# Layer 2's relus moved behind the copies of the group two ahead, and the second map's weight sums moved from GpSimd to VectorE

## The chip, the cores and the metric

The kernel runs on one core of one Trainium2 chip. The metric is the time of one execution of the program on the device, in microseconds (us). The engines are named as in the profile: PE is TensorE (matrix products, with PEld for its weight loads), DVE is VectorE, ACT is ScalarE, POOL is GpSimd, SP issues most of the DMAs.

## The reference, cut to what matters

The program runs four layers over `x` of 128 x 64 x 256 values: a gated recurrent graph layer, masked attention, a graph layer with two batch norms (layer 2, counted from 0), and a three-product graph layer. Each is a residual step on the layer norm of `x`. The change touches layer 2 alone:

```python
agg = jnp.einsum('nm,bmd->bnd', A_hat, features)
x = agg.reshape(-1, d)
h = jax.nn.relu(_batchnorm(x @ W1.T + b1, g1, be1))   # 8192 tokens x 512
out = h @ W2.T + b2                                   # 8192 tokens x 256
out = _batchnorm(out, g2, be2)                        # statistics over all 8192 tokens
return out.reshape(b, n, -1)
```

Both batch norms need the statistics of all tokens before the first token can be normalized. The first norm therefore splits layer 2: the first map (`W1`) has to be finished for every token before the first relu can run, and the second map (`W2`) reads the relus.

## The kernel before, in words

The 8192 tokens are worked in 16 groups (`NG`) of 512. Activations lie with their features on the 128 partitions. A group's hidden activations after the first map are one tile `h1s[g]` of 128 x 4 x 512: four blocks `m` of 128 features each.

**First map and first norm.** `hidden` (the products of line 781, the statistics of line 792, the copy out of PSUM of line 793) ends with group 15. `bn_finish` (lines 1028 to 1052) then works block by block, on DVE except for one power on POOL: aggregate the statistics (L1036), add epsilon (L1037), raise to the power -1/2 on POOL (L1038), multiply by gamma (L1046), compute the shift (L1047). The four blocks come one after another, since the last statistics come one block after another. `n1sc` and `n1sh` are the scale and the shift of the first norm.

**The weight sums.** Groups 4 to 12 (`SEVEN_FC2`) compute the second map as a 2 x 2 block product in seven instead of eight products. This needs four sums or differences of blocks of `w2`, written into the room of `w1`, which is free once the first map is done. `sums` (line 217) makes them, before on POOL, in line 1110, issued after the last power of the first norm.

**Relus.** `activate(g)` (lines 1144 to 1150) applies scale, shift and relu in place on ACT: four instructions of 128 x 512 for a group.

**Second map, ordinary groups** (0 to 3 and 13 to 15). Eight products per group on PE (L1182) into two PSUM banks; DVE takes the statistics of each bank (L1191), ACT copies it to SBUF (`evicted`, L1188).

**Second map, groups 4 to 12** (`second_linear`, which calls `seven`). The seven products (L1131) use four PSUM banks. Products 1, 5, 6 and 7 come first. ACT copies the first two banks, L173 for product 1 and L174 for product 5. Product 2 is then accumulated into the first bank, so it waits for L173; product 3 waits for L174. DVE adds (L176, L177, L185, L189), POOL adds one block (L180), ACT evicts one (L225), and DVE takes statistics (L1174). DVE also makes four differences of the relu results for the next group (`fc2_differences`, L1123), into one set of four blocks `ts` that each group overwrites.

**Order.** Every engine runs its own instructions in a fixed order. A scheduler sets it when the program is built, from readiness and source order. `tc.issue_after(i)` puts what is recorded inside it behind instruction `i` on the same engine. At group 12 `layer3_weights` asks for the next layer's weights by DMA (L1081 to L1087), into tiles of finished groups.

Of the kernel before, what the change touches and what calls it, by code (L numbers as in the profile page):

```python
# [10 lines left out]
ALU = mybir.AluOpType  # L11
# [9 lines left out]
NG = NTOK // GN  # L21
# [17 lines left out]
def adj_preln_kernel(ctx: ExitStack, tc: tile.TileContext, x_in, adj, vec, bg0, bg1,  # L39
                     wg0, wg1, wih, whh, wqkv, w1t, w2t, l3w1, l3w2, l3w3, out):  # L40
    nc = tc.nc
# [27 lines left out]
    mhalf = const.tile([P, GT], F32, tag="mhalf", name="mhalf")  # L69
# [6 lines left out]
    vecs = const.tile([P, V_N], F32, tag="vecs", name="vecs")  # L76
# [87 lines left out]
    def seven(products, banks, p1, p5, out, end, parts=lambda b: [b]):  # L164

        ps = banks  # L170
        for i, p in zip((1, 5, 6, 7), ps):
            products[i](p, True)
        nc.scalar.copy(p1, ps[0])  # L173
        nc.scalar.copy(p5, ps[1])  # L174

        nc.vector.tensor_tensor(p1, p1, ps[2], ALU.add)  # L176
        added = nc.vector.tensor_tensor(p5, p5, ps[3], ALU.add)  # L177

        def finish():
            nc.gpsimd.tensor_tensor(out=out[1][1], in0=p1, in1=p5, op=ALU.add)  # L180
            end(1, 1, None)
            products[2](ps[0], False)
            end(0, 0, ps[0])
            products[3](ps[1], False)
            nc.vector.tensor_tensor(out[0][1], p1, ps[1], ALU.add)  # L185
            end(0, 1, None)
            products[4](ps[3], False)
            for to, p, q in zip(*(parts(b) for b in (out[1][0], p1, ps[3]))):
                last = nc.vector.tensor_tensor(to, p, q, ALU.add)  # L189
                end(1, 0, None, to)  # L190
            return last.ins

        finish.behind = added.ins
        return finish

    def each_behind(behind, i):
        return tc.issue_after(behind[i].ins) if behind else nullcontext()
# [10 lines left out]
    def sums(eng, a11, a12, a21, a22, s1, s2, s3, s4, behind=None, which=range(4)):  # L208

        ops = (  # L210
            (s1, a21, a22, ALU.add), (s2, s1, a11, ALU.subtract),
            (s3, a11, a21, ALU.subtract), (s4, a12, s2, ALU.subtract),
        )
        for i in which:
            s, p, q, op = ops[i]
            with each_behind(behind, i):
                last = eng.tensor_tensor(out=s, in0=p, in1=q, op=op)
        return last.ins
# [64 lines left out]
    with tc.tile_pool(name="lw", bufs=5) as lw:  # L283
# [6 lines left out]
        with tc.tile_pool(name="gw", bufs=1) as gw, tc.tile_pool(name="gcn", bufs=2) as gp, \  # L290
# [5 lines left out]
            for k in range(2):  # L296
                nc.sync.dma_start(
                    out=xs[0][:, 2 * k : 2 * k + 2, :], in_=x_view[:, 2 * k : 2 * k + 2, :]
# [205 lines left out]
        with tc.tile_pool(name="back", bufs=1, reuse_waits="tile") as back_pool, \  # L504
# [196 lines left out]
            for p, nk in ((1, 8), (2, 8), (3, 7), (4, 8)):  # L701
# [7 lines left out]
                for j in range(0, len(units), 2):  # L709
# [6 lines left out]
                    if j + 2 == len(units):  # L716
# [5 lines left out]
                        else:  # L722
                            w_att = weight_tile()
                            nc.sync.dma_start(
                                out=w_att[:, :, 0:768], in_=wqkv.rearrange("(c p) f -> p c f", p=P)
# [27 lines left out]
    def arena(pool):  # L753
        return pool.tile([P, 4, GN], F32, tag="arena", name="arena")
# [44 lines left out]
    with tc.tile_pool(name="att", bufs=2, reuse_waits="tile") as ap_:  # L799
# [5 lines left out]
        def queries_keys(b):  # L805


            q, k = qk = [ap_.tile([P, 2, GN], F32, tag=t, name=t, bufs=1) for t in ("q", "k")]
            p15 = ap_.tile([P, 2, 2, HN], F32, tag="p15", name="p15", bufs=1)

            def product(w, x):
                def issue(ps, first):
                    for r in range(2):
                        nc.tensor.matmul(  # L814
                            ps[:, r, :], lhsT=w[:, r * P : (r + 1) * P], rhs=x,
                            start=first and r == 0, stop=True, skip_group_check=True,
                        )

                return issue

            out = [[d[:, :, n * HN : (n + 1) * HN] for n in range(2)] for d in qk]
            finish = seven(
                sevens(wqk_blocks, b, product), [bank((P, 2, HN)) for _ in range(4)],
                p15[:, 0], p15[:, 1], out, ends_in(out, AF.Copy),
            )
            return q, k, finish
# [109 lines left out]
        last = None  # L936
        for g in range(NG):
# [12 lines left out]
            q, k, finish = queries_keys(blocks)  # L950
# [31 lines left out]
            if last is not None:  # L982
                pss = attend(eT, v_last)
# [13 lines left out]
            last = (e_next[0], ri_next, v)  # L997
# [20 lines left out]
        pss = attend(eT, v_last)  # L1018
# [4 lines left out]
    ar_left = ctx.enter_context(tc.tile_pool(name="arena_l", bufs=NG // 2 - 1, reuse_waits="tile"))  # L1023
    outs = []

    powers = []

    def bn_finish(st, n, v_0, v_g, v_b, tag, biased=True):


        scs, shs = [], []
        for m in range(n):
            mv = bp.tile([P, 2], F32, tag=f"{tag}mv{m}", name=f"{tag}mv{m}")
            sc = bp.tile([P, 1], F32, tag=f"{tag}sc{m}", name=f"{tag}sc{m}")
            sh = bp.tile([P, 1], F32, tag=f"{tag}sh{m}", name=f"{tag}sh{m}")
            nc.vector.bn_aggr(mv, st[:, m].rearrange("p g s -> p (g s)"))  # L1036
            nc.vector.tensor_scalar(sc, mv[:, 1:2], BN_EPS, None, ALU.add)  # L1037
            powers.append(nc.gpsimd.tensor_tensor(out=sc, in0=sc, in1=mhalf[:, 0:1], op=ALU.pow))  # L1038
            mean = mv[:, 0:1]

            nc.vector.tensor_scalar(
                mean, mean, vecs[:, v_0 + m : v_0 + m + 1], -1.0, ALU.add, ALU.mult
            )
            if not biased:
                nc.vector.tensor_tensor(mean, mean, vecs[:, v_0 + m : v_0 + m + 1], ALU.add)
            nc.vector.tensor_tensor(sc, sc, vecs[:, v_g + m : v_g + m + 1], ALU.mult)  # L1046
            nc.vector.scalar_tensor_tensor(  # L1047
                sh, mean, sc, vecs[:, v_b + m : v_b + m + 1], ALU.mult, ALU.add
            )
            scs.append(sc)  # L1050
            shs.append(sh)
        return scs, shs
# [4 lines left out]
    for g in range(1, NG):  # L1057
# [10 lines left out]
        if g == 3:  # L1068
            for a in range(2):
                nc.sync.dma_start(  # L1070
                    out=w2[a], in_=w2t.rearrange("(a b p) f -> a p b f", a=2, p=P)[a]
# [33 lines left out]
    SEVEN_FC2 = range(4, NG - 3)  # L1105
    fc2_a = [[w2[c][:, :, m * P : (m + 1) * P] for c in range(2)] for m in range(2)]

    fc2_s = [w1[:, :, i * P : (i + 1) * P] for i in range(4)]
    with tc.issue_after(powers[-1].ins):
        sums(nc.gpsimd, *fc2_a[0], *fc2_a[1], *fc2_s)  # L1110

    def fc2_blocks(a):
        return [
# [3 lines left out]
    def fc2_differences(a, which=range(4)):  # L1117
        (b11, b12), (b21, b22) = fc2_blocks(a)
        t1, t2, t3, t4 = ts
        ops = ((t1, b12, b11), (t3, b22, b12), (t2, b22, t1), (t4, b21, t2))  # L1120
        for i in which:
            t, p, q = ops[i]
            nc.vector.tensor_tensor(t, p, q, ALU.subtract)  # L1123
# [20 lines left out]
    def activate(g):  # L1144
        a = h1s[g]
        for m in range(4):
            nc.scalar.activation(  # L1147
                a[:, m, :], a[:, m, :], AF.Relu,
                bias=sh1[m], scale=sc1[m],
            )  # L1150

    for g in range(NG):
        a = h1s[g]
        if g not in SEVEN_FC2:
            activate(g)

        if g % 2 == 0:
            outs.append(arena(ar_right))
        o = outs[-1][:, 2 * (g % 2) : 2 * (g % 2) + 2, :]
        if g + 1 == SEVEN_FC2[0]:  # L1160
            tt = arena(ar_right).rearrange("p i (c n) -> p i c n", c=2)
            ts = [tt[:, i] for i in range(4)]
        ahead = g + 1 in SEVEN_FC2
        if g in SEVEN_FC2:
            finish = second_linear(a, o)
            if g + 2 in SEVEN_FC2:
                activate(g + 2)
            if ahead:
                fc2_differences(h1s[g + 1], range(3))
            finish()  # L1170
            if ahead:
                fc2_differences(h1s[g + 1], [3])
            for m in range(2):
                nc.vector.bn_stats(st2[:, m, g, :], o[:, m, :])  # L1174
        else:
            pss = [bank() for _ in range(2)]
            order = [(c, m) for c in range(4) for m in range(2)]
            if g == NG - 1:

                order.sort(key=lambda cm: cm[1])  # L1180
            for c, m in order:
                nc.tensor.matmul(  # L1182
                    pss[m], lhsT=w2[c // 2][:, c % 2, m * P : (m + 1) * P], rhs=a[:, c, :],
                    start=(c == 0), stop=(c == 3),
                )

            def evicted(m):
                nc.scalar.copy(o[:, m, :], pss[m])  # L1188

            for m in range(2):  # L1190
                nc.vector.bn_stats(st2[:, m, g, :], pss[m])  # L1191
                if (g, m) != (NG - 1, 1):
                    evicted(m)
            if g + 2 in SEVEN_FC2:
                activate(g + 2)
            if ahead:
                fc2_differences(h1s[g + 1])
        if g == NG - 4:
            w_three = layer3_weights()
# [255 lines left out]
    for g in range(NG + 1):  # L1455
# [10 lines left out]
        if s3 is not None:  # L1466
            pss = [bank((P, 2, D)) for _ in range(2)]
            if g == NG:
                pss = [pss, [bank((P, 2, D)) for _ in range(2)]]
# [78 lines left out]
```

## Time and profile before

| | us |
|---|---|
| median of 3 runs | 2468.98 (2467.39 to 2470.3) |
| the profiled execution's own time | 2469.3 |
| its span, first to last instruction | 2467.5 |
| PE busy | 2446.4 (99% of the span) |
| DVE busy | 1549.2 (63%) |
| ACT busy | 1141.8 (46%) |
| POOL busy | 451.7 (18%) |

Layer 2's second map lies between about 1569 and 1681 us of the span. The span begins at the first instruction and ends with the last; the remaining 1.8 us of the execution lie around it. A matrix product of fp32 data appears in the trace as two records, so a 128x512 product takes two records of about 0.43 us each.

In a timeline a row gives the start, the duration, the engine, the line, the operation, what it writes and reads, how often it occurs in a row, and in brackets how long the engine had been idle before it and which engine's instruction ended that. The durations of neighbouring instructions on one engine overlap at their ends, so the distance between two starts is shorter than the duration of one.

### The profile page before, as it was taken

How to read it: one execution, taken by the hardware profiler on the slowest of the kernel's cores; microseconds unless marked ns; L12 is line 12 of the kernel's file. 1: busy time of each engine (PE TensorE's matmuls, PEld its weight loads, DVE VectorE, ACT ScalarE, POOL GpSimd, SP SyncE). 2: the span in 40 equal slices, each digit the busy share in tenths (PEclk: the TensorE clock that was granted, in tenths of full speed). 3: DMA queues.
4: the chain of work that ended last, by engine and by line, in shares of the span. 5: the costliest groups of instructions: out<-in, count | busy, mean ns of one | idle time of the engine just before them, and what ended most of it. 6: DMA issues, size and time to landing. Idle time of an engine off the chain costs nothing.

```text
span 2467.5 us, 46706 instructions
## 1 busy us (share of the span) xinstructions
PE 2446.4 (99%) x19756; PEld 2093.4 (85%) x19756; DVE 1549.2 (63%) x2780; ACT 1141.8 (46%) x2042; POOL 451.7 (18%) x381
## 2 busy tenths in 40 slices
PE   9999999999999999999999999999999999999999
PEld 6678888889999998888888864487998898898888
DVE  6668866666566565566599986475655445454444
ACT  4557755444354443344565566754333323333332
POOL 4432211111111111121143331023111111111110
PEclk9999999999999999999999999999999999999999
DMA  3200000001000000000122110010000000000000
GB/s 128 92 2 1 1 18 1 1 1 35 1 1 1 1 1 1 1 13 1 39 71 72 45 36 1 1 60 1 10 10 19 10 10 19 10 10 10 19 10 18
DMA packets 48561, 48.03 MB, mean 19 GB/s; under 512 B 3680, under 2 KB 44768, under 8 KB 48352
## 3 DMA queue, kind: packets, MB, share of 16 engines
q1 hardware_dynamic: 47360, 44.23, 5.8%
q8 instruction: 155, 2.54, 0.4%
q10 hardware_dynamic: 992, 0.82, 0.1%
q14 instruction: 54, 0.44, 0.1%
HBM read 28.26 MB, written 8.39 MB: 15 GB/s over the span
## 4 chain that ended last, share of the span: by engine, by line
PE 87%; DVE 6%; ACT 3%; issue 1%; POOL 1%; DMA 1%; SPq 0%; DVEq 0%; POOLq 0%; ACTq 0%
PE ps L537 41%; PE ps L1348 16%; PE ps L1393 8%; PE ps L144 4%; PE ps L781 4%; PE ps L1312 3%; PE ps L480 2%; PE ps L456 2%; PE ps L1131 2%; PE ps L814 2%; ACT arena L1147 1%; PE ps L836 1%; PE ps L1182 1%; ACT arena L228 1%; POOL arena L180 1%
## 5 line engine op out<-in xcount | busy, mean ns | idle before, releaser
L537 PE MATMUL ps<-diff,s 128*128 128x256 f32 (+1 forms) x1824 | 393.5, 371 | 0.9 <-DVE diff L657 0.9
L1348 PE MATMUL ps<-arena 128*128 128x256 f32 x1792 | 392.4, 380 | 0.0
L1348 PEld LDWEIGHTS ps<-arena 128*128 128x128 f32 x1792 | 338.0, 190 | 53.9 <-issue 9.2
L537 PEld LDWEIGHTS ps<-diff,s 128*128 128x128 f32 x1824 | 345.9, 190 | 33.8 <-issue 1.6
L551 ACT ACTIVATE gates<-gates,lbias 128x512 f32<-128x512 f32 (+5 forms) x426 | 244.2, 621 | 203.0 <-DVE gates L185 147.1
L180 POOL TENSOR_TENSOR gates<-p 128x512 f32<-128x512 f32 (+1 forms) x115 | 149.7, 1301 | 878.6 <-DVE p L177 827.8
L537 PE MATMUL ps<-h,w 128*128 128x256 f32 (+1 forms) x1028 | 241.0, 371 | 0.0
L537 PE MATMUL ps<-diff,w 128*128 128x256 f32 (+1 forms) x1040 | 238.7, 370 | 0.0
L537 PEld LDWEIGHTS ps<-diff,w 128*128 128x128 f32 x1040 | 197.4, 190 | 18.2
L537 PEld LDWEIGHTS ps<-h,w 128*128 128x128 f32 x1028 | 194.7, 190 | 19.0 <-issue 0.5
L551 ACT ACTIVATE gates<-ps,lbias 128x256 f32<-128x256 f32 (+3 forms) x213 | 91.8, 477 | 247.0 <-PE ps L537 246.8
L180 POOL TENSOR_TENSOR arena<-arena 128x256 f32<-128x256 f32 (+1 forms) x73 | 82.1, 1125 | 587.6 <-DVE arena L177 587.6
L228 ACT ACTIVATE arena<-arena 128x512 f32<-128x512 f32 (+1 forms) x160 | 88.7, 582 | 193.7 <-POOL arena L180 101.6
L185 DVE TENSOR_TENSOR gates<-p,ps 128x512 f32<-128x512 f32 (+1 forms) x115 | 76.3, 664 | 119.5 <-PE ps L537 119.4
L1393 PE MATMUL ps<-arena 128*128 128x128 f32 x1280 | 149.7, 276 | 0.0
L1393 PEld LDWEIGHTS ps<-arena 128*128 128x128 f32 x1280 | 145.5, 192 | 1.1
L96 POOL TENSOR_TENSOR rstd<-rstd,mhalf 128x4 f32<-128x4 f32 (+1 forms) x66 | 65.9, 999 | 423.2 <-DVE rstd L95 416.5
L185 DVE TENSOR_TENSOR arena<-arena,ps 128x256 f32<-128x256 f32 (+1 forms) x73 | 43.5, 596 | 157.2 <-PE ps L1348 87.4
L176 DVE TENSOR_TENSOR p<-p,ps 128x512 f32<-128x512 f32 (+1 forms) x131 | 86.7, 662 | 48.9 <-PE ps L537 47.9
L537 PE MATMUL ps<-state,w 128*128 128x256 f32 (+1 forms) x512 | 116.1, 370 | 0.9 <-ACT p L173 0.8
L189 DVE TENSOR_TENSOR gates<-p,ps 128x512 f32<-128x512 f32 (+1 forms) x115 | 76.7, 667 | 63.9 <-PE ps L537 63.2
L537 PE MATMUL ps<-state,s 128*128 128x256 f32 (+1 forms) x512 | 115.8, 369 | 0.0
(192 smaller groups left out, 4115.7 us busy)
## 6 DMA issues: line engine op xcount, KB each, us to landing
x<-in_x SPq DMA_DIRECT2D x27, 512.0 KB, 4.1
v<-vt SPq DMA_DIRECT2D x128, 64.0 KB, 2.1
out<-x SPq DMA_DIRECT2D x15, 512.0 KB, 2.9
w<-in_wih SPq DMA_DIRECT2D x4, 1024.0 KB, 7.9
w<-in_whh SPq DMA_DIRECT2D x3, 1024.0 KB, 5.1
arena<-in_l3w SPq DMA_DIRECT2D x3, 1024.0 KB, 5.1
w<-in_wqkv SPq DMA_DIRECT2D x1, 768.0 KB, 4.4
x<-in_x SPq DMA_DIRECT2D x2, 256.0 KB, 3.0
```

The lines of the kernel that those rows point to most:

```text
L144: last = nc.tensor.matmul(pss[b][half * 64 : half * 64 + 64, c, t, :], lhsT=src[rows, t, col : col + 64], rhs=a2[rows, :], start=True, sto ...
L176: nc.vector.tensor_tensor(p1, p1, ps[2], ALU.add)
L180: nc.gpsimd.tensor_tensor(out=out[1][1], in0=p1, in1=p5, op=ALU.add)
L185: nc.vector.tensor_tensor(out[0][1], p1, ps[1], ALU.add)
L189: last = nc.vector.tensor_tensor(to, p, q, ALU.add)
L228: nc.scalar.activation(o, o, func)
L537: nc.tensor.matmul(ps[:, r], lhsT=wc[:, j, :], rhs=bc, start=first and r == 0 and c == 0, stop=True, skip_group_check=True,)
L551: nc.scalar.activation(o, ps, func, bias=lbias[:, col : col + 1])
L781: nc.tensor.matmul(ps, lhsT=w1[:, c, m * P : (m + 1) * P], rhs=a[:, 2 + c, :], start=(c == 0), stop=(c == 1),)
L1312: nc.tensor.matmul(ps[:, t, :], lhsT=w[:, t * P : (t + 1) * P], rhs=b, start=first and t == 0, stop=True, skip_group_check=True,)
L1348: nc.tensor.matmul(ps[:, r, :], lhsT=w[:, c, col : col + P], rhs=b[:, c, :], start=first and r == 0 and c == 0, stop=c == 1, skip_group_ch ...
L1393: nc.tensor.matmul(ps[:, t, :], lhsT=w[:, c, t * P : (t + 1) * P], rhs=b[:, c, :], start=first and t == 0 and c == 0, stop=c == 3, skip_gr ...
```

## The change

The relus of groups 0 and 1 are recorded ahead of the loop. All others are recorded two groups ahead: those of group g+2 behind the second copy out of PSUM of group g, which is L1188 in an ordinary group and L174 in a group with seven products. The second copy is kept in `finish.copied` or in `last` for that. The four weight sums go to DVE, behind the last shift of the first norm. No computation is added or left out.

```diff
-        nc.scalar.copy(p5, ps[1])
+        copied = nc.scalar.copy(p5, ps[1])
...
+        finish.copied = copied.ins
...
-            powers.append(nc.gpsimd.tensor_tensor(out=sc, in0=sc, in1=mhalf[:, 0:1], op=ALU.pow))
+            nc.gpsimd.tensor_tensor(out=sc, in0=sc, in1=mhalf[:, 0:1], op=ALU.pow)
...
-            nc.vector.scalar_tensor_tensor(
-                sh, mean, sc, vecs[:, v_b + m : v_b + m + 1], ALU.mult, ALU.add
+            shifts.append(
+                nc.vector.scalar_tensor_tensor(
+                    sh, mean, sc, vecs[:, v_b + m : v_b + m + 1], ALU.mult, ALU.add
+                )
             )
...
-    with tc.issue_after(powers[-1].ins):
-        sums(nc.gpsimd, *fc2_a[0], *fc2_a[1], *fc2_s)
+    with tc.issue_after(shifts[-1].ins):
+        sums(nc.vector, *fc2_a[0], *fc2_a[1], *fc2_s)
...
+    for g in range(2):
+        activate(g)
     for g in range(NG):
         a = h1s[g]
-        if g not in SEVEN_FC2:
-            activate(g)
...
             finish = second_linear(a, o)
-            if g + 2 in SEVEN_FC2:
+            with tc.issue_after(finish.copied):
                 activate(g + 2)
...
             def evicted(m):
-                nc.scalar.copy(o[:, m, :], pss[m])
+                return nc.scalar.copy(o[:, m, :], pss[m])
...
                 if (g, m) != (NG - 1, 1):
-                    evicted(m)
-            if g + 2 in SEVEN_FC2:
-                activate(g + 2)
+                    last = evicted(m)
+            if g + 2 < NG:
+                with tc.issue_after(last.ins):
+                    activate(g + 2)
```

More of the change, by code (lines that the diff above doesn't have):

```diff
@@ L1024, in adj_preln_kernel @@
     outs = []
-    powers = []
+    shifts = []
     def bn_finish(st, n, v_0, v_g, v_b, tag, biased=True):
```

## The prediction

> **What bounds the kernel now.** I read the shares first: PE is busy 99% of the span, so only a gap in PE counts. Then I asked which of PE's waits lie in the second map of layer 2 (1569 to 1681 us). The view of waits names all of them, with total, count and longest in us:
>
> ```profile
> PE ps L1182 <- ACT arena L1147: 1.4, 1, 1.4
> PE ps L1131 <- ACT arena L173: 1.3, 1, 1.3
> ```
>
> There are just two gaps, 2.8 us together: 0.11% of the time. That caps any gain from better order here. The busy time by stretch (columns: stretch, length, busy us of PE, PEld, DVE, ACT, POOL with counts, clock, DMA) shows where they lie, and that PE is full in the rest, at full clock:
>
> ```profile
> 1569.00:1582.00 13.00, 11.55 (x27) 4.78 (x26) 8.44 (x24) 7.92 (x12) 4.77 (x8) 1.00 0.01 1
> 1582.00:1604.00 22.00, 22.00 (x52) 9.69 (x51) 7.28 (x11) 22.00 (x34) 0.21 (x1) 1.00 0.00 0
> 1604.00:1609.00 5.00, 3.68 (x18) 2.86 (x16) 1.52 (x4) 5.00 (x10) 0.00 (x0) 1.00 0.01 2
> 1609.00:1660.20 51.20, 51.20 (x237) 45.10 (x238) 42.79 (x83) 26.16 (x51) 12.37 (x13) 1.00 0.22 72
> ```
>
> The timeline of the first gap, all engines:
>
> ```profile
> 1578.80 0.55 POOL L1038 TENSOR_TENSOR n1sc<-n1sc,mhalf 128x1 f32<-128x1 f32 x1 [1.95 <-DVE n1sc L1037]
> ...
> 1579.31 2.89 POOL L217 TENSOR_TENSOR w<-w 128x256 f32<-128x256 f32 x4
> 1579.38 0.67 DVE L1046 TENSOR_TENSOR n1sc<-n1sc,vecs 128x1 f32<-128x1 f32 x1 [0.54 <-POOL n1sc L1038]
> 1580.09 0.65 DVE L1047 SCALAR_TENSOR_TENSOR n1sh<-n1mv,n1sc,vecs 128x1 f32<-128x1 f32 x1
> 1580.77 2.93 ACT L1147 ACTIVATE arena<-arena,n1sh,n1sc 128x512 f32<-128x512 f32 x4 [2.05 <-DVE n1sh L1047]
> ...
> 1581.63 1.55 PE L1182 MATMUL ps<-arena,w 128*128 128x512 f32 x3 [1.45 <-ACT arena L1147]
> ```
>
> PE waits for the relu of group 0's last block, which waits for the last shift. That shift is late because L1046 and L1047 are slow. The same two take 0.16 and 0.22 us for the other three blocks (the tile views give medians of 160 and 220 ns, maxima of 672 and 647). Each ends just as one of the POOL sums ends: four take 2.89 us, so the first ends near 1580.03, the second near 1580.75.
>
> The second gap:
>
> ```profile
> 1601.25 5.76 ACT L1147 ACTIVATE arena<-arena,n1sh,n1sc 128x512 f32<-128x512 f32 x8
> ...
> 1604.06 3.62 PE L1131 MATMUL ps<-arena,w 128*128 128x256 f32 x16
> ...
> 1604.26 0.70 DVE L1191 BATCH_NORM_STATS2 st<-ps 128x6 f32<-128x512 f32 x1 [0.16 <-PE ps L1182]
> ...
> 1606.90 0.59 ACT L1188 COPY arena<-ps 128x512 f32<-128x512 f32 x1
> 1607.37 0.84 ACT L1147 ACTIVATE arena<-arena,n1sh,n1sc 128x512 f32<-128x512 f32 x1
> 1608.08 0.59 ACT L1188 COPY arena<-ps 128x512 f32<-128x512 f32 x1
> 1608.55 0.39 ACT L173 COPY arena<-ps 128x256 f32<-128x256 f32 x1
> ...
> 1608.99 3.29 PE L1131 MATMUL ps<-arena,w 128*128 128x256 f32 x14 [1.32 <-ACT arena L173]
> ```
>
> Product 1 of group 4 has long been in its bank, but L173 stands in ACT's queue behind eight relus for later groups and group 3's two copies. ACT is full from 1582 to 1609 with relus that nobody needs yet.
>
> **What the Trainium skill says.** "SBUF — State Buffer", section "SBUF: two separate sides": the port pair shared by VectorE and GpSimd is an exclusive lock held for a whole instruction, also against a VectorE operation with two SBUF inputs; the loser blocks. L1046 and L1047 have two SBUF inputs, and the trace agrees: 0.67 and 0.65 us against 0.16 and 0.22. "PSUM — Partial Sum Buffer", section "Engine vs sequencer instructions": ScalarE's queue is strict FIFO. The trace agrees: L173 waits 1.3 us past PE's need behind relus. The same page, "PSUM bank collisions raise a hardware error": readers on two engines of one bank must be kept apart. Here L1188 starts only once L1191 has ended (1666.98 after 0.70 us from 1666.24).
>
> **Part 1, the sums.** POOL loses four instructions of 0.72 us and becomes idle there. DVE gains four of 128x256. The nearest DVE row is L217 on an arena tile of that shape, four in 1.62 us (1691.90), 0.40 each; a row of twice the size takes 0.68, which bounds it at 2.7 us. Removed: (0.67 - 0.16) + (0.65 - 0.22) = 0.94 us before the shift. The shift then ends at 1579.80, the relu starts at 1579.83 (ACT is idle from 1578.73), PE restarts at 1580.69. The gap falls from 1.45 to 0.51 us; what is late next is the chain of the shift itself. The DVE sums lie at 1579.83 to 1581.45. The next DVE work, group 0's first statistics, moves to 1582.80 - 0.94 = 1581.86, so they hide. At 2.7 us the statistics would come 0.7 us late, and with them group 0's copies and the relus of group 2. These have 2.7 us to spare (below). Cost nothing, gain 0.94.
>
> **Part 2, the relus.** Their number (64) and durations stay; only their place changes. On ACT everything behind a relu of group g+2 now waits for group g's second copy.
>
> *Ordinary groups.* PE takes 6.87 us per group (statistics of L1191 at 1582.80, 1589.66, 1596.53). A group's second copy ends about 1.3 us after the group's last product, and four relus take 4 x 0.706 = 2.83 us (eight in 5.65), so they are done 4.15 us after the end of group g and are needed 6.87 us after it. Slack 2.7 us, no gap. Group 4's four differences on DVE (0.60 to 0.65 each) wait for the last relu of group 4, 4.15 us after the end of group 2, and end 6.0 us after it, just as group 3's first statistics are due (6.87 - 0.86 = 6.0). At worst a tenth there, and the second statistics, which set the next step, are not moved.
>
> *Group 4, where the second gap is.* All times less 0.94. Products 1, 5, 6, 7 start at 1603.12 and take 16 x 0.216 = 3.46, to 1606.58. Group 3's last statistics start at 1603.32, its last copy at 1604.05, and with 0.47 us to the next start the relus of group 5 start at 1604.52. L173 is behind them: 1604.52 + 2.83 = 1607.35, and PE sees it 0.44 later (1608.55 to 1608.99), at 1607.79. With the old PE order that would leave 1.2 us of gap and gain a tenth. But the order of the built program differs: group 5's product 1 and the first half of its product 5 (six records, 1.30 us) now stand in front of group 4's product 2. They carry PE to 1607.88. Their own needs: the second relu of group 5 (1604.52 + 1.41 + 0.12 = 1606.05) and the difference t1 (DVE, 0.65 later, 1606.75, needed at 1607.44). Both are there. Product 2 finds L173 done with 0.09 us to spare, product 3 needs L174 at about 1608.05 and is due at 1608.74. The gap of 1.32 goes. With the margin so thin, part of it may stay; the full 1.2 us only if the six records themselves are late.
>
> *Groups 5 to 12.* PE takes 28 x 0.216 = 6.05 us per group. ACT has L173, L174, four relus and L225: 0.28 + 0.26 + 2.83 + 0.27 = 3.64. DVE has four additions of 0.34, two statistics of 0.61 and four differences of 0.60: 4.98. After the relus L225 falls some 5.3 us into its group instead of 4.5; its reader is the statistics (L1174), and its bank is needed again only at the second next group. L173 of the next group is due 3.46 us into it, and ACT is free by then. No gap, as before.
>
> *Groups 13 to 15.* Relus of 14 follow L174 of 12, those of 15 the copies of 13, done 4.15 us into group 14. Slack 2.7 us again.
>
> *Downstream.* The DMAs for layer 3 wait for the last additions (L189) of finished groups, so they, and the POOL work behind them that ends 1.33 us before POOL's first power of the second norm, move with PE. Layer 3 keeps its instructions and order.
>
> **Sum.** 0.94 + 1.32 = 2.26 us. The profiled execution goes from 2469.3 to 2467.04 (its span from 2467.5 to 2465.24). The median of the runs shown lies 0.3 below that execution, so 2468.98 - 2.26 = 2466.7. That is 0.09%, less than the 0.2% (4.9 us) that a measurement of this kernel can tell from no change.
>
> **Rivals.**
> *The copy stays late (16%).* Relus of group 5 still precede L173, and t1 or the six hoisted records come late. For it: the margins of 0.09 and 0.7 us. Against: every need was placed with measured steps. Only the 0.94 remains: 2468.0.
> *Nothing moves (6%).* The DVE sums or a downstream wait takes the gain: 2469.0. Against: 0.4 us of DVE cover, 2.7 us of slack behind it, and no absolute time downstream.
> *Slower: VectorE becomes the bound in groups 5 to 12 (4%).* Differences now follow relus that are only one group old, and POOL's L180 (1.1 us) can lock DVE out of each group: 4.98 + 1.1 = 6.08 us, 0.03 over PE's 6.05. It decides once DVE needs more than 6.05 us a group; for a loss of 0.2% it has to lose 7.2 us over eight groups, 0.9 each, giving 2473.9. For it: DVE is busy 42.79 of 51.20 us. Against: DVE carries that same work and lock now without a gap on PE.
> *Faster by more than 0.2% (3%).* The two gaps hold 2.8 us; more would need a gain outside this stage, for which I see no place.
>
> **How the numbers follow.** Both gaps as reckoned: 71%. Within 0.2% fall this case, the late copy and nothing moving, 93%; faster 3%, slower 4%. The range takes the cap of 2.8 us plus the spread of the runs (1.6 us below their median) at its low end, 2464.7, and no gain at its high end, 2469.1.
>
> **What would show it.** Right: L1046 and L1047 of the last block at 0.16 and 0.22 us; the first gap near 0.5 us; no wait of L1131 for L173; the end of group 12's products near 1657.9 instead of 1660.2. Wrong: PE waiting for L173, for L1147 or for DVE's differences in each group of seven products, or POOL's layer 3 work ending after the second norm's power is wanted.

## The result, and the profile after

The changed kernel takes 2465.70 us, the median of 22 runs (2464.13 to 2467.1). The kernel before, run beside it, takes 2469.01 us (22 runs, 2467.39 to 2471.09). The ratio is 0.9986, with a 95% interval of 0.9980 to 0.9992: 3.3 us less, somewhere from 2.0 to 4.9. The profiled execution has a span of 2463.8 us against 2467.5.

The view of waits, PE alone, 1569 to 1700 us. Each row gives who waited for whom, the total, the count and the longest wait in us:

```profile
PE ps L144 <- ACT arena L111: 1.0, 2, 0.6
PE ps L1225 <- DVE arena L1215: 0.7, 1, 0.7
PE ps L1185 <- ACT arena L1150: 0.5, 1, 0.5
```

The wait for L173 is no longer among them, and the wait for the last relu (L1147 before, L1150 now) is 0.5 us instead of 1.4. The other rows belong to the start of layer 3 and stood there before with the same times.

The timeline of the changed kernel at the first gap, all engines:

```profile
1578.71 0.54 POOL L1039 TENSOR_TENSOR n1sc<-n1sc,mhalf 128x1 f32<-128x1 f32 x1 [1.95 <-DVE n1sc L1038]
...
1579.29 0.16 DVE L1047 TENSOR_TENSOR n1sc<-n1sc,vecs 128x1 f32<-128x1 f32 x1 [0.54 <-POOL n1sc L1039]
1579.49 0.22 DVE L1049 SCALAR_TENSOR_TENSOR n1sh<-n1mv,n1sc,vecs 128x1 f32<-128x1 f32 x1
1579.62 1.55 DVE L218 TENSOR_TENSOR w<-w 128x256 f32<-128x256 f32 x4
1579.74 2.22 ACT L1150 ACTIVATE arena<-arena,n1sh,n1sc 128x512 f32<-128x512 f32 x3 [1.11 <-DVE n1sh L1049]
...
1580.61 1.98 PE L1185 MATMUL ps<-arena,w 128*128 128x512 f32 x4 [0.51 <-ACT arena L1150]
...
1581.77 0.70 DVE L1194 BATCH_NORM_STATS2 st<-ps 128x6 f32<-128x512 f32 x1 [0.60 <-PE ps L1185]
```

The multiplication and the shift (L1047 and L1049, before L1046 and L1047) are back at 0.16 and 0.22 us. The sums take 1.55 us on DVE, and DVE then still idles 0.60 us before the first statistics.

The same view at the second gap:

```profile
1603.03 9.24 PE L1134 MATMUL ps<-arena,w 128*128 128x256 f32 x42
...
1603.96 0.59 ACT L1191 COPY arena<-ps 128x512 f32<-128x512 f32 x1 [0.18 <-DVE st L1194]
1604.44 2.93 ACT L1150 ACTIVATE arena<-arena,n1sh,n1sc 128x512 f32<-128x512 f32 x4
1605.99 0.69 DVE L1126 TENSOR_TENSOR arena<-arena 128x512 f32<-128x512 f32 x1 [2.07 <-ACT arena L1150]
1607.27 0.35 ACT L173 COPY arena<-ps 128x256 f32<-128x256 f32 x1
```

PE has 42 records on end where the kernel before had 16 and then a pause. L173 starts at 1607.27, 1.28 us earlier than before. The busy times by stretch (stretch, length, then busy us of PE, PEld, DVE, ACT and POOL with counts, clock, DMA) show how the cover changed:

```profile
1581.00:1603.00 22.00, 22.00 (x52) 9.69 (x51) 7.49 (x12) 12.94 (x20) 0.00 (x0) 1.00 0.00 0
1603.00:1657.40 54.40, 54.40 (x253) 47.75 (x252) 43.93 (x86) 38.09 (x69) 12.76 (x13) 1.00 0.21 68
```

ACT, which was full for the 22 us ahead of group 4, is now busy 12.94 us there, and more in the groups with seven products. PE has no gap from 1580.61 on. DVE's busy time and the clock are about as before.

**A measure for the stage.** Whole spans differ for reasons outside the change: in a second profile of the kernel before, the second map begins 0.7 us later (1575.41 against 1574.67). So I compare the distance from the first product of the second map to the place where the chain of work that ended last reaches layer 3's second weights (L1348 before); in every kernel that place lies 0.16 us behind the start of the line's first record. It is 130.34 us before and 127.81 after: 2.53 us less.

### The profile page after: what moved, and what is told of

It is laid out like the page before. It is cut to its first block, busy times and chain, and to the rows that moved or that the text cites. A ratio compares the mean times of both kernels' runs of the same rounds, so it can differ in the third digit from the quotient of the medians.

```text
span 2463.8 us, 46697 instructions
## 1 busy us (share of the span) xinstructions
PE 2445.8 (99%) x19756; PEld 2093.3 (85%) x19756; DVE 1549.5 (63%) x2784; ACT 1142.2 (46%) x2042; POOL 449.3 (18%) x377
## 4 chain that ended last, share of the span: by engine, by line
PE 88%; DVE 7%; ACT 2%; issue 1%; POOL 1%; DMA 1%; SPq 0%; ACTq 0%; DVEq 0%; POOLq 0%
PE ps L538 41%; PE ps L1352 16%; PE ps L1397 8%; PE ps L782 4%; PE ps L144 4%; PE ps L1316 3%; PE ps L457 2%; PE ps L481 2%; PE ps L1134 2%; PE ps L1185 2%; PE ps L815 1%; PE ps L837 1%; ACT arena L229 1%; DVE st L92 1%; POOL arena L180 1%
```

## The experiments

Times are medians of 10 to 21 runs, of 4 for one group ahead. The ratio comes with its interval from the comparison of the runs and can differ from the quotient of the two medians by some units of its last digit. "Stage" is that distance, in one profiled execution of each kernel; the kernel before gave 130.34 and 130.31 in two, the changed kernel 127.81 and 127.80, so it repeats within 0.03 us.

| kernel | time | before, beside it | ratio, 95% interval | stage |
|---|---|---|---|---|
| sums alone | 2467.01 | 2468.86 | 0.9992 (0.9984 to 1.0000) | 129.38 |
| relus alone | 2465.81 | 2468.86 | 0.9989 (0.9983 to 0.9996) | 128.75 |
| both, group 5 kept behind group 4 | 2466.96 | 2468.86 | 0.9993 (0.9984 to 1.0001) | 129.11 |
| changed kernel again | 2465.56 | 2469.08 | 0.9985 (0.9978 to 0.9991) | 127.80 |
| interleaved groups 0 and 1 | 2464.91 | 2469.08 | 0.9983 (0.9976 to 0.9989) | 127.03 |
| sums five times | 2465.70 | 2469.08 | 0.9986 (0.9979 to 0.9993) | 127.90 |
| one group ahead | 2485.86 | 2469.08 | 1.0068 (1.0054 to 1.0081) | 147.09 |
| before again | 2469.46 | 2469.25 | 1.0000 (0.9991 to 1.0009) | 130.31 |
| before, four writes added | 2467.66 | 2469.25 | 0.9996 (0.9988 to 1.0004) | 130.32 |

### The sums alone

```diff
 # the kernel before, with
-    with tc.issue_after(powers[-1].ins):
-        sums(nc.gpsimd, *fc2_a[0], *fc2_a[1], *fc2_s)
+    with tc.issue_after(shifts[-1].ins):
+        sums(nc.vector, *fc2_a[0], *fc2_a[1], *fc2_s)
```

> Only the weight sums go to VectorE behind the last shift; the relus stay as in the kernel before. Theory (two separate gaps): L1046 and L1047 of the last block fall back to 0.16 and 0.22 us, PE's first gap falls from 1.45 to about 0.5 us, and the second gap, product 2 of group 4 waiting for L173, stays at 1.3 us because ScalarE starts its run of relus 0.94 us earlier too. Gain 0.94 us, about 2468.0. Rival (ScalarE's run is pinned elsewhere): the second gap grows to 2.2 us and nothing is gained.

PE's waits in this kernel:

```profile
PE ps L1133 <- ACT arena L173: 1.3, 1, 1.3
...
PE ps L1184 <- ACT arena L1149: 0.5, 1, 0.5
```

The first gap shrinks, the second is untouched, and the stage loses 0.96 us against 0.94 reckoned. The rival, a second gap of 2.2 us, is out. The median of the whole time fell by 1.85 us, 0.9 more than the stage, though the interval of the ratio ends at no change; this excess comes back below.

### The relus alone

```diff
 # the changed kernel, with
-    with tc.issue_after(shifts[-1].ins):
-        sums(nc.vector, *fc2_a[0], *fc2_a[1], *fc2_s)
+    with tc.issue_after(powers[-1].ins):
+        sums(nc.gpsimd, *fc2_a[0], *fc2_a[1], *fc2_s)
```

> Only the relus are tied behind the copies; the sums stay on GpSimd. Theory: the first gap stays at 1.45 us with L1046 and L1047 of the last block at 0.67 and 0.65 us, and the second gap is gone. Gain 1.3 us of idle time plus 0.26 us of restart (the end of the record before the gap overlaps nothing, and the first record after it is longer), 1.58 us, about 2467.4. Rival (without the earlier shift the copy L173 stays late): a gap of some tenths before product 2 of group 4.

The timeline of this kernel at the first gap:

```profile
1578.65 2.90 POOL L218 TENSOR_TENSOR w<-w 128x256 f32<-128x256 f32 x4
1578.72 0.67 DVE L1047 TENSOR_TENSOR n1sc<-n1sc,vecs 128x1 f32<-128x1 f32 x1 [0.54 <-POOL n1sc L1039]
1579.43 0.65 DVE L1048 SCALAR_TENSOR_TENSOR n1sh<-n1mv,n1sc,vecs 128x1 f32<-128x1 f32 x1
1580.11 2.22 ACT L1148 ACTIVATE arena<-arena,n1sh,n1sc 128x512 f32<-128x512 f32 x3 [2.04 <-DVE n1sh L1048]
1580.97 1.55 PE L1183 MATMUL ps<-arena,w 128*128 128x512 f32 x3 [1.44 <-ACT arena L1148]
```

With the sums on POOL the two small DVE instructions are slow again, to the hundredth, so the POOL sums are what makes them slow. That they do it by the lock that the prediction names is not seen in a trace by itself. It fits: here too the two end with the first and the second POOL sum (1579.39 and 1580.08; four sums in 2.90 us from 1578.65). The stage loses 1.59 us, as expected. 0.96 and 1.59 make 2.55, and both together gave 2.53: the parts are independent. The whole time again fell further than the stage, by 3.05 us.

### Both, with group 5 kept behind group 4

```diff
 # the changed kernel, with
-            finish = second_linear(a, o)
+            with tc.issue_after(products_done[0].ins) if g == SEVEN_FC2[0] + 1 else nullcontext():
+                finish = second_linear(a, o)
```

`products_done[0]` is the last product issued, here the last of group 4.

> The changed kernel, but group 5's products are kept behind the last product of group 4, so that the six records no longer stand in front of product 2 of group 4. Theory (the hoisted records carry PE over the wait): L173 still stands behind the four relus of group 5, PE waits 1.0 us for it, and with the restart the time is 1.2 us above the changed kernel, 2466.9. Rival (having fewer relus in front of L173 is what closes the gap): no gap, 2465.7.

```profile
1602.30 3.62 PE L1136 MATMUL ps<-arena,w 128*128 128x256 f32 x16
...
1603.23 0.59 ACT L1194 COPY arena<-ps 128x512 f32<-128x512 f32 x1 [0.17 <-DVE st L1197]
1603.71 2.93 ACT L1152 ACTIVATE arena<-arena,n1sh,n1sc 128x512 f32<-128x512 f32 x4
...
1606.54 0.35 ACT L173 COPY arena<-ps 128x256 f32<-128x256 f32 x1
...
1606.94 3.29 PE L1136 MATMUL ps<-arena,w 128*128 128x256 f32 x14 [1.03 <-ACT arena L173]
```

PE waits 1.03 us for L173, and the stage is 1.30 us longer than in the changed kernel (1.2 expected). So tying the relus brought L173 forward by only 0.3 us measured against PE's need; the rest of the gap was filled by the six records of group 5 that the scheduler put ahead of product 2. In the changed kernel product 2 is the 23rd record, due at 1603.03 + 22 x 0.216 = 1607.78, and it starts then. L173 ends at 1607.62, and PE restarts 0.05 us after that copy where it does wait (1606.54 + 0.35 against 1606.94 above), so about 0.1 us was to spare.

The reverse was not run: the six records put ahead while the relus stay where they were. From the trace of the kernel before, the 23rd record would be due there at 1604.06 + 22 x 0.216 = 1608.81, and PE could go on after L173 at 1608.99. By this estimate the new order on PE alone would have left some 0.2 us of the gap of 1.32.

### The changed kernel again

> The changed kernel once more, to stand beside the next three on the same chip. Theory (both gaps, restart included, 2.5 us): the span's last matrix products begin 2.6 us earlier than before and the ratio lies near 0.9990. Rival (another 1.1 us was gained at the very end, where the last output lands): the distance from the last VectorE addition to the end of the span is again 1.1 us shorter than in the kernel before.

The stage repeats at 127.80. The end of the program is shorter again: the last two outputs are issued from 3.5 us before the end on, as in the first profile, where the kernel before has 4.6. So a part of the time is gained after all of layer 3's arithmetic.

### Groups 0 and 1 interleaved

```diff
 # the changed kernel: products (group, block) of groups 0 and 1, two for each pair (cut)
+    for i, c in ((0, 0), (0, 1), (0, 2), (1, 0), (1, 1), (0, 3), (1, 2), (1, 3)):
+        for m in range(2):
+            nc.tensor.matmul(two[i][m], ...)
```

> The changed kernel, with the first two blocks of group 1's products put in front of the last block of group 0's. Theory (the remaining gap of 0.5 us is PE waiting for the last relu of group 0 alone): those four products, 3.4 us, cover it, PE has no gap from the first map to the end of the second, and the time falls by 0.5 us plus 0.26 us of restart, 0.8 us, to about 2464.9. Rival (group 0's copies and with them the relus of group 2 come 3.0 us later and too late): a new gap at group 2, no gain.

The timeline of PE in this kernel:

```profile
1574.43 14.09 PE L1160 MATMUL ps<-arena,w 128*128 128x512 f32 x32
1588.35 13.90 PE L1192 MATMUL ps<-arena,w 128*128 128x512 f32 x32
1602.08 1.24 PE L1134 MATMUL ps<-arena,w 128*128 128x256 f32 x5
```

No bracket is left: PE has no gap. The stage loses another 0.77 us. This version is the fastest measured, 2464.91 us beside 2465.56 of the changed kernel on the same chip. The difference of 0.65 us fits the stage's, but it is smaller than what the intervals of the two ratios can tell apart; it rests on the profile.

### The sums five times

The same four values are written five times over. Some of the repeats the scheduler placed between and behind the first statistics.

```diff
-        sums(nc.vector, *fc2_a[0], *fc2_a[1], *fc2_s)
+        for _ in range(5):
+            sums(nc.vector, *fc2_a[0], *fc2_a[1], *fc2_s)
```

> The changed kernel with the four sums made five times over on VectorE (the same values written again), 16 more instructions of 0.39 us, 6.2 us. Theory (the sums hide behind PE with wide cover): group 0's statistics come some 4 us late, group 2's first relu at about 1588.6 is still in time for 1589.2, no new gap, time as the changed kernel. Rival (the cover is only the 0.4 to 0.6 us between the sums and the first statistics): a gap before group 2 of several us.

```profile
1579.23 5.23 DVE L218 TENSOR_TENSOR w<-w 128x256 f32<-128x256 f32 x15
...
1580.21 12.28 PE L1186 MATMUL ps<-arena,w 128*128 128x512 f32 x28 [0.51 <-ACT arena L1151]
1584.38 0.69 DVE L1195 BATCH_NORM_STATS2 st<-ps 128x6 f32<-128x512 f32 x1
...
1586.52 2.93 ACT L1151 ACTIVATE arena<-arena,n1sh,n1sc 128x512 f32<-128x512 f32 x4
```

Group 0's first statistics come 3.0 us later than in the changed kernel (measured from PE's restart: 4.17 against 1.16 us), and group 2's relus start 3.1 us later (6.31 against 3.23). PE still has no new gap; the stage grew by 0.09 us. The expected 4 us was too much, since only fifteen of the twenty sums stood ahead of the first statistics, and they took 5.23 us, 0.35 each. The cover of the sums is thus at least 3 us.

### One group ahead instead of two

```diff
-    for g in range(2):
+    for g in range(1):
         activate(g)
...
             with tc.issue_after(finish.copied):
-                activate(g + 2)
+                activate(g + 1)
...
-            if g + 2 < NG:
+            if g + 1 < NG:
                 with tc.issue_after(last.ins):
-                    activate(g + 2)
+                    activate(g + 1)
```

> The changed kernel with the relus tied behind the copies of the group one ahead instead of two. Theory (a group's relus follow its predecessor's copies by 0.8 us for the first block, and the copies end 1.3 us after the products): PE waits about 2.1 us at the start of groups 1, 2, 3, 14 and 15 and about 4 us in group 4, nothing in groups 5 to 13; with restarts 16 us, about 2482. Rival (the distance hardly matters because the next group can start on its first block): under 2 us lost in all.

```profile
PE ps L1185 <- ACT arena L1150: 11.1, 6, 2.1
PE ps L1134 <- ACT arena L1150: 2.1, 1, 2.1
...
PE ps L1134 <- ACT arena L173: 0.7, 1, 0.7
```

The gaps came where expected, 2.12 us each at groups 1, 2, 3, 14 and 15, and none in groups 5 to 13. At group 4 it was 2.12 + 0.74 instead of 4. Yet the stage grew by 19.3 us, not 16. The new idle time is 5 x 2.12 + 2.12 + 0.74 = 13.5 us, and seven restarts at 0.26 make 1.8. The busy times by stretch of this kernel show the rest:

```profile
1594.40:1603.70 9.30, 7.13 (x16) 2.96 (x16) 1.40 (x2) 4.04 (x8) 0.00 (x0) 1.00 0.00 0
1603.70:1614.60 10.90, 8.83 (x16) 3.55 (x16) 1.40 (x2) 3.94 (x7) 0.00 (x0) 0.84 0.00 0
1679.80:1689.10 9.30, 7.13 (x16) 2.96 (x16) 1.40 (x2) 4.04 (x8) 8.78 (x6) 1.00 0.00 0
1689.10:1697.90 8.80, 8.76 (x16) 3.53 (x16) 2.01 (x7) 3.30 (x6) 0.57 (x1) 0.81 0.00 0
```

Twice in the course of the gaps the granted clock falls, to a mean of 0.84 and 0.81 in these stretches, and the same 16 records take 1.7 us longer. That is another 3.4 us; 13.5 + 1.8 + 3.4 = 18.7, and 0.6 stays open. In none of the other ten profiles does the clock fall between the first 20 us and the last 5, so the gaps are the likely reason. The trace does not show why it fell after these gaps (the one before group 3, the one before group 15) and not after the others.

### The end of the program

The stage explains 2.53 of 3.3 us. In the two profiles at hand the rest lay after the last outputs had been issued. The DMA records offered one difference: a packet of queue 14, which fetches instructions, lay among the last output packets in the kernel before. In all the others it was 2 us or more away on one side or the other. Its place follows the number of VectorE instructions in the program. With four and two fewer than in the kernel before it comes 2.5 and 2.0 us after the start of the last output packet; in the kernel before 0.3 us ahead of it; with three to five more some 7.5 us ahead, with nineteen more 20 us ahead. Two kernels tested this: the kernel before, and the kernel before with four writes to an unused column, which are four instructions more:

```diff
-            nc.vector.scalar_tensor_tensor(
+            shift = nc.vector.scalar_tensor_tensor(
...
+            if tag == "n1" and m == 3:
+                with tc.issue_after(shift.ins):
+                    for _ in range(4):
+                        nc.vector.memset(rsum, 0.0)
```

> The kernel before, unchanged, profiled a second time. In its first profile the last output DMA was issued 4.6 us before the end of the span, in all the other kernels 3.5 us, and one packet of queue 14, which fetches instructions, lay among the last output packets there and nowhere else. Theory (where that packet falls follows from the number of VectorE instructions, 3524 here): the distance is 4.6 us again. Rival (chance of one execution): 3.5 us.

> The kernel before with four writes of one column into a constant no longer used, on VectorE behind the last shift of the first norm, where it is idle for 2 us; relus and sums as before. Theory (the instruction fetch of VectorE's queue collides with the last output; four more instructions move it forward by some 7 us): both gaps of the second map stay at 1.4 and 1.3 us, the distance from the last output's issue to the end falls from 4.6 to 3.5 us, and the time falls by 1.1 us to about 2467.9. Rival (the end's length is chance): the median stays at 2469.0.

The DMA view from 2454 to 2470 us (GB/s in slices of 0.4 us; then queue 14, with its packets, MB and share of the DMA engines' time), first of the kernel before in its second profile:

```profile
GB/s 0 0 0 0 0 0 0 0 0 0 0 0 0 0 0 0 0 0 0 0 0 0 0 0 0 87 330 346 341 205 23 0 0 0 0 0 0 0 0 0
...
q14 instruction: 1, 0.01, 0.1%
```

and with the four writes:

```profile
GB/s 0 0 0 0 0 0 20 0 0 0 0 0 0 0 0 0 0 0 0 0 0 228 341 341 338 64 0 0 0 0 0 0 0 0 0 0 0 0 0 0
...
q14 instruction: 1, 0.01, 0.1%
```

In the second the one packet of queue 14 stands alone in the seventh slice, 6 us ahead of the outputs. In the first it falls among them. The same view from the issue of the very last output on gives its size and the us from issue to landing, again of the kernel before (from 2464.3 us):

```profile
out<-x ACTq DMA_DIRECT2D x1, 128.0 KB, 2.9
```

and with the four writes (from 2462.6 us):

```profile
out<-x ACTq DMA_DIRECT2D x1, 128.0 KB, 1.9
```

So it is the last output alone that lands late: after 3.0 and 2.9 us in the two profiles of the kernel before, after 1.9 us in every other kernel. The outputs ahead of it take 1.7 to 1.9 us in all of them, and what follows its landing takes 1.0 us in all. The stage and both its gaps stay with the four writes (130.32, 1.4 and 1.3 us). So the end of the kernel before is 1.1 us longer each time, and four VectorE instructions more take that away.

The time fell by 1.6 us in the median, but the interval of the ratio includes 1; the profiles carry the finding. The medians agree with it as a whole: in the seven kernels of the table that have the short end, one group ahead left aside since its clock differs from run to run (0.996 to 0.999), they fell by 0.7 to 1.6 us more than the stage, by 1.05 on the mean. That the packet is what delays the landing is inferred from where it lies. No run moved it alone, and how one packet can cost that much was not shown.

## Why the prediction was right, and where it was off

- *Part 1, the sums.* As reckoned: 0.94 us expected, 0.96 measured alone. That the POOL sums slow the two instructions is shown from both sides, by taking them away and by putting them back. The lock between the two engines is the reason that fits their durations.
- *The DVE sums hide.* Right: five times the sums cost 0.09 us, with group 0's statistics 3.0 us late. That is what 0.4 us of cover and 2.7 us of slack behind it allow.
- *Part 2, the second gap.* The mechanism was right, the products put ahead included. L173 came with about 0.1 us to spare where 0.09 was reckoned. Without the products put ahead 1.03 us of gap stays, close to the 1.2 named. So three quarters of this gap were closed by the order on PE, which the scheduler changed along with the relus.
- *The size of the second gap.* Mis-sized. I took the idle time, 1.32 us, as the cost; removing it gave 1.59. The record before a gap ends 0.16 us later than the next one would have started, since records overlap when PE runs on, and the first record after the gap takes 0.48 us where the others take 0.38. So a gap that vanishes gives its idle time and 0.26 us. Part 1 only shortened its gap and gave just the difference.
- *Downstream.* "Layer 3 keeps its instructions and order" holds, and layer 3 moved as a whole. But I took the end of the program to be fixed, and it became 1.1 us shorter: with three more VectorE instructions an instruction fetch no longer falls among the last output packets, and the last output lands 1.1 us sooner. This term was missing from the sum. With both corrections it is 0.96 + 1.59 + 1.1 = 3.65 us in the profiles, against 3.7 between the spans and 3.3 between the medians. The medians' 3.3 is more than the 2.8 us that the prediction took as the most that this stage could give. That the result still lies in its range is in part luck: the low end had another 1.6 us for the spread of the runs, and the missing terms used some of it.
- *The rivals.* The late copy did not happen; the run with group 5 kept behind group 4 shows what it would have cost. The relus in front of L173 and L226 (L225 before) in groups 5 to 12 cost nothing, and VectorE did not become the bound: PE is busy 54.40 of 54.40 us there.
- *The forecast of no measurable change* by the bound of 0.2% holds: the change is 0.14%. But the bound was wider than the measurement: with 22 runs of each kernel the interval of the change, 0.08 to 0.20%, leaves out zero.

## What to carry to other kernels

A stall can be cheap to remove where the engine that causes it is full with work nobody needs yet: find the latest point at which each group's work is still in time, and tie it there. Two groups ahead left 2.5 us to spare here (group 2's last relu ends at 1586.77, the group's first product starts at 1589.29), and one group ahead cost 20 us. Then read the order of the built program: here six records that the scheduler had put ahead closed 1.0 us of the second gap, and the earlier copy 0.3. And look for GpSimd work beside short VectorE instructions on the critical path: here two of them lost 0.51 and 0.43 us, each less than one GpSimd instruction of 0.72 us.

## What was not expected of the hardware

- With repeated gaps of 2.1 us on PE its granted clock fell for a while, twice in one stage, at 1.7 us each, on top of the idle time.
- Where an instruction fetch fell among the last output packets, the last output landed 1.1 us later. The place of the fetch moved with the number of VectorE instructions, so a change elsewhere in the program gained this microsecond without touching the end.
